# Fewer sums on TensorE, two scratch tiles for the dots and a shorter one-hot in a sparse graph attention layer

## The chip, the cores and the metric

The kernel runs on one core of a Trainium2 chip. The metric is the device time of one execution in microseconds (us). Several executions were timed, and one more was recorded by the hardware profiler; all times inside an execution come from that record and count from its first instruction.

## The reference

Input `x` has 3327 rows of 1024 fp32 values, `adj` is a 3327 x 3327 matrix of 0 and 1 (int32) with ones on its diagonal and few ones elsewhere (the chance of an edge is 0.0024 in each direction). The three weights are 1024 x 1024.

```python
h = jnp.maximum(_layernorm(x, axis=-1), 0.0)
f = h @ Wf + bf
g = h @ Wg + bg
e = relu(f @ g.T)
scores = jnp.where(adj > 0, e, NEG)
attention = softmax(scores, axis=1)
out = x + attention @ (h @ W + bW)
```

## The kernel before

Only the neighbours of a row count, since all other scores are NEG. The kernel uses two identities: `f @ g.T` equals `(h A + v) . h` for a product `A = Wf Wg^T` made once (with the biases in `v` and in one more column), and `attention @ (h W)` equals `(attention @ h) W`. So each row needs a query `q = h A + v` (TensorE), a dot product of `q` with the row `h` of each neighbour (VectorE), a softmax over these few scores, the weighted sum `y` of the same neighbour rows, and `y W`.

**First part (to about 237 us).** `adj` and `x` are streamed tile by tile (128 rows). ScalarE counts degrees, GpSimd multiplies `adj` by column numbers, VectorE extracts the neighbour lists with its max-of-8 operation, ScalarE normalizes `x` to `h`, and SP stores `h` (`hd`), the lists (`pd`) and the candidates (`cd`) to DRAM. TensorE computes `A` meanwhile. Rows are then sorted by degree: a one-hot of the rank's low seven bits (`ohp`, L1064 to L1073) is multiplied on TensorE with the high bits and gives the permutation `perm`, so that a tile holds rows of like degree. The one-hot is built in three pieces on VectorE, with the int32 `lo` and the fp32 `iotap` as operands, and the 26 matmuls follow piece by piece. After the second piece the last two tiles of `h` are scaled and stored, and the load of the last two of eight 512 KB pieces of `W_sb` is queued on SP. Then two gathers on GpSimd fetch the `h` rows of the first two tiles (`hps`, L1092), and the queries of these tiles are made (L1108 to L1122): three `bank` matmuls, transposes, and `third`, which makes 342 columns of `q` in 16 passes. After that come the last lists and stores.

**Second part.** The 26 tiles run in the order `ORDER`; tile t has `CAPS[ORDER[t]]` neighbour slots (37 down to 11, in all 468). The slots of a tile come in one or two chunks (`split`). The steps of a tile, with the functions that issue them (L1200 to L1344):

- `L`, `G`, `H`: GpSimd gathers the list, one 512 KB block of neighbour rows per slot k into one of 26 buffers `G`, and the tile's own rows. `H` is transposed (`turned`, `hc`) and multiplied with `A` (`third`, then `qc` copies to `q`, and `fq` refills the PSUM bank).
- `d` (L1247): one VectorE operation multiplies a neighbour block by `q` and accumulates the score of slot k. It also has to write the 128 x 1024 products somewhere: the tile `junk`, one for all dots. The operation is two instructions, the product and a read of the accumulator.
- `S`, `A`, `E`, `Y`, `T`: maximum, exponentials and sum of a chunk; `Y` scales slot 0, which becomes the running sum `y`.
- The weighted sum of the other slots goes two ways. On VectorE, `s` (L1299) does `y = G_k * w_k + y`. On TensorE, `w` (ScalarE) scales the block in place, and `p` (L1295) adds its transpose into PSUM by eight 128 x 128 transposes. `SHARE[t]` says how many slots of tile t go to TensorE (`on_tensor`), in all 185. At the end `yt` adds the transpose of `y` to the same PSUM banks, column half by column half, and `yc` copies to `yT`.
- `fo`, `W`, `rc`, `X`, `O`: bias, the projection on TensorE (32 passes), scaling, the added `x` and the scatter to the output.

The order on each engine in this part is written out by a planner in Python (`steps_of`, `forward`, `backward`, `planned`). `steps_of` lists every step with its engine, the time it takes and lasts, and what it depends on; `forward` plays the list with priorities, each engine taking the step of best rank (VectorE with a penalty `TURNS` for a second step of the same kind), and `backward` makes new ranks from the latest times. Of 30 passes with random jitter `WIDE` the best is kept, and the kernel issues the steps in the order of their planned start times. The semaphores between the engines come from the tiles that are read and written, not from the plan.

Of the kernel before, what the change touches and what calls it, by code (L numbers as in the profile page):

```python
# [10 lines left out]
FP = mybir.dt.float32  # L11
# [20 lines left out]
ORDER = [24, 15, *range(15), *range(16, 24), 25]  # L32
SHARE = [10, 12, 18, 13, 11, 10, 11, 9, 8, 8, 9, 9, 6, 9, 5, 4, 5, 4, 3, 3, 3, 2, 3, 0, 6, 4]
ONE_CHUNK = 18
# [7 lines left out]
SEED = 1  # L42
WIDE = 0.6
LAG = 2
# [284 lines left out]
def steps_of():  # L329
# [9 lines left out]
    for t, s in enumerate(ORDER):  # L339
# [3 lines left out]
        if t > 1:  # L343
            add("POOL", 1.31, 1.31, ("H", t), row=True)
            add("DMA", 1.33, 3.2, ("Hd", t), ("H", t))
            for g in range(2):
                add("PE", 0.44, 0.66, ("hT", t, g), ("Hd", t), ("hc", t - 1, g), ("hT", t, g - 1), frees=[("H", t)] * g)
            for g in range(2):
                add("ACT", 0.49, 0.6, ("hc", t, g), ("hT", t, g), *(("q", t - 1, i, j) for i in range(3) for j in range(QS)))
            for i in range(3):  # L350
                for j in range(QS):
                    add(
                        "PE", 4.66 / QS, 4.66 / QS + 0.2, ("q", t, i, j), ("hc", t, 0), ("hc", t, 1), ("fq", 3 * t + i),
                        ("q", t, i, j - 1),
                    )
                add(
                    "ACT", 0.4, 0.52, ("qc", t, i), ("q", t, i, QS - 1),
                    *(("d", t - 2, k) for k in range(CAPS[ORDER[t - 2]])),
                )
                if 3 * t + i + 2 < 3 * n:  # L360
                    add("ACT", 0.38, 0.48, ("fq", 3 * t + i + 2), ("qc", t, i))
# [6 lines left out]
        if t == n - 1:  # L368
            add("POOL", 1.31, 1.31, ("x", t), row=True)
            add("DMA", 1.33, 3.2, ("xd", t), ("x", t))  # L370
        summed = []
        for c, (k0, k1) in enumerate(ends):
            last = c == len(ends) - 1
            for k in range(k0, k1):
                late = [("F", t)] if k >= KL else [("hc", 2, 1) if k < 6 else ("qc", 2, 1)] if t == 1 else []
                add("POOL", 1.31, 1.31, ("G", t, k), ("Ld", t), *late, row=True)
                add("DMA", 1.33, 3.2, ("Gd", t, k), ("G", t, k))
                add(
                    "DVE", 1.2, 1.38, ("d", t, k), ("Gd", t, k), *(("qc", t, i) for i in range(3)),
                    ("M", t), at=(256.0, 266.0)[t] if t < 2 else 0.0,  # L380
                )
# [9 lines left out]
            for k in range(max(k0, 1), k1):  # L391
                if k in on_tensor(t):
                    add("ACT", 1.05, 1.15, ("w", t, k), ("E", t, c))
                    add("PE", 0.873, 1.07, ("p", t, k), ("w", t, k), ("yc", t - 1, 0), ("yc", t - 1, 1), frees=[("G", t, k)])
                    summed.append(("p", t, k))
                else:
                    add("DVE", 1.2, 1.28, ("s", t, k), ("E", t, c), ("Y", t, c), frees=[("G", t, k)])
                    summed.append(("s", t, k))
        for o in range(2):
            add("ACT", 0.62, 0.72, ("fo", t, o), ("rc", t - 1, o), ("T", t, len(ends) - 1))  # L400
        for g in range(2):
            add(
                "PE", 0.44, 0.66, ("yt", t, g), *summed, ("Y", t, len(ends) - 1), ("yc", t - 1, 0), ("yc", t - 1, 1),
                ("yt", t, g - 1),
                frees=[("G", t, 0)] * g,
            )
        for g in range(2):
            add("ACT", 0.49, 0.6, ("yc", t, g), ("yt", t, g), *(("W", t - 1, o, j) for o in range(2) for j in range(WS)))
        for o in range(2):
            for j in range(WS):  # L410
                add(
                    "PE", 7.0 / WS, 7.0 / WS + 0.2, ("W", t, o, j), ("yc", t, 0), ("yc", t, 1), ("fo", t, o),
                    ("W", t, o, j - 1),
                )
# [16 lines left out]
def forward(steps, rows, noise=None, fixed=None):  # L431
# [19 lines left out]
    while events:  # L451
# [7 lines left out]
        for e in FREE_AT:  # L459
# [24 lines left out]
            if e == "PE" and now < 480:  # L484
                takes, lasts = takes * 1.12, lasts * 1.12
            if e == "DVE":
                if k.name[0] in "ds" and k.name[0] == done:
                    takes, lasts = takes + 0.12, lasts + 0.12
                done = k.name[0]
# [86 lines left out]
def edge_path(ctx: ExitStack, tc: tile.TileContext, x, adj, Wf, bf, Wg, bg, W, bW, out, flag):  # L576
# [67 lines left out]
    with ExitStack() as part1:  # L644
# [212 lines left out]
        with tc.manual_schedule(engines={  # L857
# [59 lines left out]
            for i in range(NT - 3):  # L917
                degrees(i + 2)
                keys(i + 2, nc.gpsimd)
                if i == NT - 4:  # L920
                    degrees(NT - 1)
                    keys(NT - 1, nc.gpsimd)
                if i < 3:
                    for c in (2 * i + 2, 2 * i + 3):
                        transposed(WgT[:, :, c * P : (c + 1) * P], A_sb[:, c, :D])
                        empty()
# [91 lines left out]
            slots = slots.rearrange("p (t s) -> p t s", s=NT)  # L1018
            ohp = kpool.tile([P, N], FP, name="r").bitcast(BF)[:, : NT * P].rearrange("p (t d) -> p t d", d=P)

# [18 lines left out]
            lo = c1.tile([P, NT], I32, name="lo")  # L1039
            nc.vector.tensor_scalar(lo, ranki, P - 1, None, op0=ALU.bitwise_and)  # L1040
            measured(22, False)
            rooted(22)
# [20 lines left out]
            ps = p_mm.tile([P, CB], FP, name="ps_A")  # L1063
            for t0, t1 in ((0, 10), (10, 20), (20, NT)):  # L1064
                nc.vector.tensor_tensor(
                    ohp[:, t0:t1, :], lo[:, t0:t1, None].to_broadcast([P, t1 - t0, P]),
                    iotap[:, None, :].to_broadcast([P, t1 - t0, P]), op=ALU.is_equal,
                )
                for t in range(t0, t1):
                    nc.tensor.matmul(  # L1070
                        ps[:, : 2 * NT], ohp[:, t, :], place[:, t, :, :].rearrange("p a s -> p (a s)"),
                        start=(t == 0), stop=(t == NT - 1),
                    )  # L1073
                if t1 == 20:
                    inverted(late)
                    scaled(late)
                    store_h(late)
                    inverted(last)
                    scaled(last)
                    store_h(last)  # L1080
                    for k in range(6, KD):
                        load_W(k)
            listed(NT - 3)
# [25 lines left out]
            hTs = [wT.tile([P, KD, P], FP, name="WfT") for s in ORDER[:2]]  # L1109
            pq = [bank(i, True) for i in range(3)]  # L1110
            transposed(hTs[0], hps[0])
            empty()
# [19 lines left out]
            store_lists(last, NT)  # L1132
            store_left(last)

            over = c1.tile([P, 1], FP, name="over")
# [21 lines left out]
    with tc.manual_schedule(engines={  # L1157
# [9 lines left out]
        res = tiles("xp", 2, [P, O])  # L1167
        junk = tiles("junk", 1, [P, D], BF)[0]
        scs = tiles("sc", 3, [P, KM])
# [77 lines left out]
        def dot(t, k):  # L1247
            q = qs[t % 2]
            nc.vector.tensor_tensor_reduce(  # L1249
                junk, row(t, k), q[:, :D], 1.0, 0.0, op0=ALU.mult, op1=ALU.add,  # L1250
                accum_out=scs[t % 3][:, k : k + 1],
# [46 lines left out]

        def s(t, k):  # L1299
            y = row(t, 0)  # L1300
            nc.vector.scalar_tensor_tensor(y, row(t, k), scs[t % 3][:, k : k + 1], y, op0=ALU.mult, op1=ALU.add)  # L1301

# [98 lines left out]
```

## Time and profile before

| | |
|---|---|
| median of 3 executions (lowest, highest) | 1243.65 us (1237.1, 1246.98) |
| the profiled execution: its time, its span | 1243.08 us, 1241.3 us |
| TensorE busy, share of the span | 1117.1 us, 90% |
| VectorE (DVE) busy | 1108.0 us, 89% |
| GpSimd (POOL) busy | 895.3 us, 72% |
| ScalarE (ACT) busy | 618.3 us, 50% |
| read from HBM, over the span | 344.11 MB, 301 GB/s |
| mean granted TensorE clock | 0.953 |

The profile has several views. The slices cut the span into 40 parts of 31 us and give each engine's busy share in tenths; PEclk is the clock granted to TensorE in tenths of full speed. A line of the groups gives a source line, engine and operation, the tiles as out<-in, shapes, the count, busy time and mean ns of one, and then the idle time of the engine just before these instructions with what ended it. A line of the timeline gives start, duration, engine, source line, operation, tiles and, in brackets, the idle time before it and its releaser. PE is TensorE's matmuls, PEld its weight loads. The ends of matmuls are modelled, so that a busy TensorE isn't TensorE at its peak.

### The profile page before, as it was taken

The page shows a single profiled execution, that of the slowest core. Times are in us where ns is not written, and L with a number is a line of the kernel's source. Part 1 is how long each engine was busy: PE and PEld are TensorE (multiplying, and loading weights), DVE is VectorE, ACT ScalarE, POOL GpSimd, SP SyncE. Part 2 cuts the span into 40 slices and gives each one's busy share as a digit, 9 for nine tenths or more (in the row PEclk, how much of TensorE's full clock was granted, in tenths as well). Part 3 has the DMA queues.
Part 4 walks back from the last instruction along what each step waited for, and adds up shares of the span by engine and source line. Part 5 has one row for each costly group of instructions (what it writes and reads, how often), then busy time and mean ns, then how long its engine had stood idle before and what let it go on. Part 6 is the DMA issues. An engine that isn't in the chain of part 4 may idle for free. (4 is left out here: it accounts for less than half of the span.)

```text
span 1241.3 us, 14490 instructions
## 1 busy us (share of the span) xinstructions
PE 1117.1 (90%) x4632; PEld 712.1 (57%) x4632; DVE 1108.0 (89%) x2169; ACT 618.3 (50%) x941; POOL 895.3 (72%) x676
## 2 busy tenths in 40 slices
PE   2799980779998899999999999999999999999995
PEld 1566650447647466566666676665666565655553
DVE  5999997638898989988999999998999999999991
ACT  6899988216526275346543565453323433333250
POOL 8999994355676777776777777657777887777721
PEclk8799995789998899999999999999999999999998
DMA  9999999677868999998999989779988999899842
GB/s 368 419 396 397 403 344 354 199 297 265 293 222 271 312 338 303 316 324 294 303 337 332 310 292 330 274 248 317 319 289 274 317 305 319 267 313 314 301 137 53
DMA packets 101916, 374.46 MB, mean 302 GB/s; under 512 B 14859, under 2 KB 18602, under 8 KB 98631
## 3 DMA queue, kind: packets, MB, share of 16 engines
q0 software_dynamic: 79584, 286.77, 68.8%
q1 hardware_dynamic: 22246, 86.68, 18.5%
q8 instruction: 38, 0.62, 0.2%
q14 instruction: 48, 0.39, 0.1%
HBM read 344.11 MB, written 29.30 MB: 301 GB/s over the span
## 5 line engine op out<-in xcount | busy, mean ns | idle before, releaser
L635 POOL DMA_INDIRECT G<-hd,ps x454 | 535.8, 1180 | 207.1 <-issue 99.3
L1249 DVE CUSTOM_DVE_ANT_0 junk<-G,q 128x1024 bf16<-128x1024 f32 x468 | 573.4, 1225 | 58.1 <-ACT q L1120 26.8
L1316 PE MATMUL p_o<-W_sb,yT 128*128 128x512 f32 x832 | 365.4, 594 | 1.1 <-ACT yT L1312 0.9
L1236 PE MATMUL p_q<-A_sb,hT 128*128 128x342 f32 x1152 | 356.5, 459 | 6.6 <-ACT hT L1232 2.9
L1301 DVE SCALAR_TENSOR_TENSOR G<-G,sc 128x1024 f32<-128x1024 f32 x257 | 330.8, 1287 | 9.2 <-ACT G L1274 4.1
L1236 PEld LDWEIGHTS p_q<-A_sb,hT 128*128 128x128 f32 x1152 | 215.8, 193 | 113.3 <-issue 15.1
L1316 PEld LDWEIGHTS p_o<-W_sb,yT 128*128 128x128 f32 x832 | 156.6, 190 | 190.1 <-issue 183.7
L1289 PE MATMUL p_y<-ident,G 128*128 128x128 f32 x1688 | 207.2, 274 | 15.8 <-issue 10.9
L1289 PEld LDWEIGHTS p_y<-ident,G 128*128 128x128 f32 x1688 | 190.0, 141 | 47.1 <-issue 25.4
L1285 ACT ACTIVATE G<-G,sc 128x1024 f32<-128x1024 f32 x185 | 197.2, 1138 | 0.1
L700 POOL TENSOR_TENSOR r<-r,iotaj 128x1664 f32<-128x1664 f32 (+3 forms) x50 | 183.7, 3729 | 3.9 <-ACT r L693 3.9
L1327 ACT ACTIVATE xp<-p_o,rs 128x512 f32<-128x512 f32 x50 | 33.0, 682 | 201.6 <-DMA out_dram<-xp,perm 97.9
L833 PE MATMUL ps_A<-WgT,WfT 128*128 128x342 f32 x432 | 129.3, 458 | 2.4 <-ACT WfT L828 2.4
L763 DVE MAX8 cand<-r 128x8 f32<-128x208 f32 (+2 forms) x416 | 118.9, 360 | 3.8 <-POOL r L700 3.5
L833 PEld LDWEIGHTS ps_A<-WgT,WfT 128*128 128x128 f32 x432 | 81.1, 191 | 42.3 <-ACT WfT L828 2.6
L1242 ACT COPY q<-p_q 128x342 f32<-128x342 f32 x72 | 31.7, 445 | 105.5 <-DVE sc L1249 46.8
L693 ACT ACTIVATE r<-r 128x3327 f32<-128x3327 int32 (+3 forms) x27 | 77.3, 2864 | 11.6 <-DMA r<-in_adj_dram 11.6
L1312 ACT COPY yT<-p_y 128x512 f32<-128x512 f32 x52 | 30.1, 584 | 68.9 <-PE p_y L1289 58.2
L635 POOL DMA_INDIRECT xp<-in_x_dram,perm x25 | 44.0, 1760 | 17.9 <-ACT xp L1327 11.2
L1334 POOL DMA_INDIRECT out_dram<-xp,perm x25 | 32.2, 1286 | 31.3 <-DMA xp<-in_x_dram,perm 20.7
L1232 ACT COPY hT<-p_t 128x512 f32<-128x512 f32 x48 | 27.3, 586 | 54.1 <-PE p_q L1236 23.6
L1270 ACT ACTIVATE sc<-sc,nm 128x10 f32<-128x10 f32 (+10 forms) x36 | 11.0, 305 | 81.2 <-DVE nm L1260 39.7
(144 smaller groups left out, 715.1 us busy)
## 6 DMA issues: line engine op xcount, KB each, us to landing
r<-in_adj_dram SPq DMA_DIRECT2D x24, 1663.5 KB, 12.2
xt<-in_x_dram SPq DMA_DIRECT2D x22, 512.0 KB, 13.3
hd<-xt SPq DMA_DIRECT2D x22, 512.0 KB, 10.5
G<-hd,ps POOLq DMA_INDIRECT x454
A_sb<-in_L_gnn_Wg_dram SPq DMA_DIRECT2D x8, 512.0 KB, 17.1
A_sb<-in_L_gnn_Wf_dram SPq DMA_DIRECT2D x8, 512.0 KB, 11.9
W_sb<-in_L_gnn_W_dram SPq DMA_DIRECT2D x8, 512.0 KB, 7.8
cd<-cand SPq DMA_DIRECT2D x25, 64.0 KB, 12.7
```

Of the source, the lines that this page charges most:

```text
L635: return nc.gpsimd.indirect_dma_start(out=to, out_offset=None, in_=table, in_offset=bass.IndirectOffsetOnAxis(ap=idx, axis=0), **kw,)
L693: nc.scalar.activation(r[:n, b:e], a[:n, b:e], AF.Sign, accum_out=to)
L700: eng.tensor_mul(r[:n, b:e], r[:n, b:e], iotaj[:n, b:e])
L763: nc.vector.max(cands[t][:n, s * 8 : s * 8 + 8], r[:n, s * SW : min(N, (s + 1) * SW)])
L833: nc.tensor.matmul(ps[:, :QB], WfTs[c][:, k, :], WgT[:, k, o : o + QB], start=(k == 0), stop=(k == KD - 1))
L1236: nc.tensor.matmul(ps_q[(3 * t + i) % 2][:, :QB], hT[:, k, :], A_sb[:, k, i * QB : (i + 1) * QB], start=False, stop=(k == KD - 1), skip_gr ...
L1249: nc.vector.tensor_tensor_reduce(junk, row(t, k), q[:, :D], 1.0, 0.0, op0=ALU.mult, op1=ALU.add, accum_out=scs[t % 3][:, k : k + 1],)
L1285: nc.scalar.activation(g, g, AF.Copy, scale=scs[t % 3][:, k : k + 1])
L1289: nc.tensor.matmul(ps_y[g][:, c, :], of[:, (4 * g + c) * P : (4 * g + c + 1) * P], ident, is_transpose=True, start=((t, g) not in begun an ...
L1301: nc.vector.scalar_tensor_tensor(y, row(t, k), scs[t % 3][:, k : k + 1], y, op0=ALU.mult, op1=ALU.add)
L1316: nc.tensor.matmul(ps_o[o], yT[:, k, :], W_sb[:, k, o * CB : (o + 1) * CB], start=False, stop=(k == KD - 1), skip_group_check=True,)
L1327: nc.scalar.activation(to, ps_o[o], AF.Copy, scale=rss[t % 3])
```

## The change

- `SHARE` moves slots from TensorE (`w` and `p`) to VectorE (`s`): the list's sum falls from 185 to 168, one slot each in 17 tiles.
- `junk` becomes `junks`, two tiles; dot k writes tile k % 2.
- In the last tile `s` works on one column half at a time, so that the transposes of the first half depend on the sums of the first half alone.
- The planner's table follows: a dot takes 1.148 in place of 1.2, the surcharge of 0.12 for two operations of a kind in a row remains for sums alone, TensorE is no longer taken as 12% slower before 480 us, `WIDE` is 0.3, and `qc` and `W` get the dependencies that the diff shows. So the order of the second part is computed anew.
- The one-hot is one operation with bf16 operands: `lob` (a bf16 copy of `lo`) against `iotaq`, a constant that GpSimd writes in the first part. Its layout has the tile index innermost, and the 26 matmuls read their weights with that stride.
- The loads of the last two pieces of `W_sb` move behind the last lists and stores.
- Six matmuls of 512 columns whose result is not used (`warm`) stand between the three `bank` matmuls and the first transposes.

```diff
-SHARE = [10, 12, 18, 13, 11, 10, 11, 9, 8, 8, 9, 9, 6, 9, 5, 4, 5, 4, 3, 3, 3, 2, 3, 0, 6, 4]
+SHARE = [9, 11, 18, 12, 10, 9, 10, 8, 7, 7, 8, 8, 5, 8, 4, 4, 4, 4, 3, 3, 3, 2, 3, 0, 5, 3]
-WIDE = 0.6
+WIDE = 0.3
...
-                    *(("d", t - 2, k) for k in range(CAPS[ORDER[t - 2]])),
+                    *(("d", t - 2, k) for k in range(CAPS[ORDER[t - 2]])), *(("S", t - 2, c) for c in range(2) if i == 2),
...
-                    "DVE", 1.2, 1.38, ("d", t, k), ("Gd", t, k), *(("qc", t, i) for i in range(3)),
+                    "DVE", 1.148, 1.32, ("d", t, k), ("Gd", t, k), *(("qc", t, i) for i in range(3)),
...
+                elif t < n - 1:
+                    add("DVE", 1.205, 1.29, ("s", t, k), ("E", t, c), ("Y", t, c), frees=[("G", t, k)])
+                    summed.append(("s", t, k))
                 else:
-                    add("DVE", 1.2, 1.28, ("s", t, k), ("E", t, c), ("Y", t, c), frees=[("G", t, k)])
-                    summed.append(("s", t, k))
+                    for g in range(2):
+                        add("DVE", 0.66, 0.74, ("s", t, k, g), ("E", t, c), ("Y", t, c), ("s", t, k, g - 1), frees=[("G", t, k)] * g)
+                        halves[g].append(("s", t, k, g))
...
-                    "PE", 7.0 / WS, 7.0 / WS + 0.2, ("W", t, o, j), ("yc", t, 0), ("yc", t, 1), ("fo", t, o),
-                    ("W", t, o, j - 1),
+                    "PE", 7.0 / WS, 7.0 / WS + 0.2, ("W", t, o, j), *(("yc", t, g) for g in range(2 * (j + 1) // WS)),
+                    ("fo", t, o), ("W", t, o, j - 1),
...
-                takes, lasts = takes * 1.12, lasts * 1.12
+                takes, lasts = takes * 1.0, lasts * 1.0
             if e == "DVE":
-                if k.name[0] in "ds" and k.name[0] == done:
+                if k.name[0] == "s" == done:
...
+                    iotaq = c1.tile([P, P, NT], BF, name="iotaq")
+                    nc.gpsimd.iota(
+                        iotaq, pattern=[[1, P], [0, NT]], base=0, channel_multiplier=0,
+                        allow_small_or_imprecise_dtypes=True,
+                    )
...
+            lob = c1.tile([P, NT], BF, name="lob")
+            nc.vector.tensor_copy(lob, lo)
...
-            for t0, t1 in ((0, 10), (10, 20), (20, NT)):
-                nc.vector.tensor_tensor(
-                    ohp[:, t0:t1, :], lo[:, t0:t1, None].to_broadcast([P, t1 - t0, P]),
-                    iotap[:, None, :].to_broadcast([P, t1 - t0, P]), op=ALU.is_equal,
+            nc.vector.tensor_tensor(
+                ohp, lob[:, None, :].to_broadcast([P, P, NT]), iotaq, op=ALU.is_equal
+            )
+            for t in range(NT):
+                nc.tensor.matmul(
+                    ps[:, : 2 * NT], ohp[:, :, t], place[:, t, :, :].rearrange("p a s -> p (a s)"),
+                    start=(t == 0), stop=(t == NT - 1),
                 )
...
-                    for k in range(6, KD):
-                        load_W(k)
...
+            warm = p_tr.tile([P, 4, P], FP, name="ps_tr").rearrange("p a b -> p (a b)")
+            for i in range(6):
+                nc.tensor.matmul(warm, ident, A_sb[:, i, :CB], start=True, stop=True)
             transposed(hTs[0], hps[0])
...
+            for k in range(6, KD):
+                load_W(k)
...
-        junk = tiles("junk", 1, [P, D], BF)[0]
+        junks = tiles("junk", 2, [P, D], BF)
...
-                junk, row(t, k), q[:, :D], 1.0, 0.0, op0=ALU.mult, op1=ALU.add,
+                junks[k % 2], row(t, k), q[:, :D], 1.0, 0.0, op0=ALU.mult, op1=ALU.add,
...
-        def s(t, k):
-            y = row(t, 0)
-            nc.vector.scalar_tensor_tensor(y, row(t, k), scs[t % 3][:, k : k + 1], y, op0=ALU.mult, op1=ALU.add)
+        def s(t, k, g=None):
+            part = slice(0, D) if g is None else slice(g * CB, (g + 1) * CB)
+            y, row_k = row(t, 0)[:, part], row(t, k)[:, part]
+            nc.vector.scalar_tensor_tensor(y, row_k, scs[t % 3][:, k : k + 1], y, op0=ALU.mult, op1=ALU.add)
```

More of the change, by code (lines that the diff above doesn't have):

```diff
@@ L370, in steps_of @@
             add("DMA", 1.33, 3.2, ("xd", t), ("x", t))
-        summed = []
+        summed, halves = [], ([], [])
         for c, (k0, k1) in enumerate(ends):
@@ L402, in steps_of @@
             add(
-                "PE", 0.44, 0.66, ("yt", t, g), *summed, ("Y", t, len(ends) - 1), ("yc", t - 1, 0), ("yc", t - 1, 1),
+                "PE", 0.44, 0.66, ("yt", t, g), *summed, *halves[g], ("Y", t, len(ends) - 1), ("yc", t - 1, 0), ("yc", t - 1, 1),
                 ("yt", t, g - 1),
@@ L1018, in edge_path @@
             slots = slots.rearrange("p (t s) -> p t s", s=NT)
-            ohp = kpool.tile([P, N], FP, name="r").bitcast(BF)[:, : NT * P].rearrange("p (t d) -> p t d", d=P)
+            ohp = kpool.tile([P, N], FP, name="r").bitcast(BF)[:, : NT * P].rearrange("p (d t) -> p d t", t=NT)
             incl = c1.tile([P, NBIN], FP, name="incl")
@@ L1063, in edge_path @@
             ps = p_mm.tile([P, CB], FP, name="ps_A")
-            for t0, t1 in ((0, 10), (10, 20), (20, NT)):
-                nc.vector.tensor_tensor(
-                    ohp[:, t0:t1, :], lo[:, t0:t1, None].to_broadcast([P, t1 - t0, P]),
-                    iotap[:, None, :].to_broadcast([P, t1 - t0, P]), op=ALU.is_equal,
-                )
[L1069 to L1080, printed above, removed]
-                    for k in range(6, KD):
-                        load_W(k)
+            nc.vector.tensor_tensor(
[5 more added lines that the diff above has]
+                    start=(t == 0), stop=(t == NT - 1),
+                )
+            inverted(late)
+            scaled(late)
+            store_h(late)
+            inverted(last)
+            scaled(last)
+            store_h(last)
             listed(NT - 3)
```

## The prediction

> **What bounds the kernel now.** I read the page's slices first, then the costliest groups, then the timeline of VectorE, of the start and of the end. The slices show no single bound:
>
> ```profile
> PE   2799980779998899999999999999999999999995
> DVE  5999997638898989988999999998999999999991
> ...
> PEclk8799995789998899999999999999999999999998
> DMA  9999999677868999998999989779988999899842
> ```
>
> TensorE and VectorE are both over 90% busy from slice 19 (570 us) to the tail, and DMA is near 90%. As PE's ends are modelled, I price its work by start distances instead: 32 projection matmuls stand between 1196.06 and 1209.90, so 0.4325 each; 48 transposes take 5.40 us with 0.27 for the last, so 0.109 each; the 342-column matmuls 0.2875. Counted in the timeline, the stretch from 570 to 1210 holds 832 matmuls of `p_q`, 614 of `p_o` and 1145 transposes: 239.2+265.6+124.8 = 629.6 us of PE in 640. VectorE, by the distances shown below, needs 310 dots x1.148 + 193 sums x1.197 + 16.2 of small operations + 121 pairs of dots x0.119 + 27 pairs of sums x0.124 = 620.9. In the same way the 290 us from 280 on hold 248 of PE and 266 of VectorE: there both wait in turn. So **PE bounds the late stage with VectorE 9 us behind it**. The groups that the change touches:
>
> ```profile
> L1249 DVE CUSTOM_DVE_ANT_0 junk<-G,q 128x1024 bf16<-128x1024 f32 x468 | 573.4, 1225 | 58.1 <-ACT q L1120 26.8
> ...
> L1301 DVE SCALAR_TENSOR_TENSOR G<-G,sc 128x1024 f32<-128x1024 f32 x257 | 330.8, 1287 | 9.2 <-ACT G L1274 4.1
> ...
> L1289 PE MATMUL p_y<-ident,G 128*128 128x128 f32 x1688 | 207.2, 274 | 15.8 <-issue 10.9
> ...
> L1285 ACT ACTIVATE G<-G,sc 128x1024 f32<-128x1024 f32 x185 | 197.2, 1138 | 0.1
> ```
>
> VectorE's timeline shows what its 98% consists of:
>
> ```profile
> 707.81 1.22 DVE L1249 CUSTOM_DVE_ANT_0 junk<-G,q 128x1024 bf16<-128x1024 f32 x1
> 708.95 0.08 DVE L1249 DVE_READ_ACCUMULATOR2_ANT sc<- 128x1 f32 x1
> 709.07 1.22 DVE L1249 CUSTOM_DVE_ANT_0 junk<-G,q 128x1024 bf16<-128x1024 f32 x1
> 710.22 0.08 DVE L1249 DVE_READ_ACCUMULATOR2_ANT sc<- 128x1 f32 x1
> 710.22 1.28 DVE L1301 SCALAR_TENSOR_TENSOR G<-G,sc 128x1024 f32<-128x1024 f32 x1
> 711.41 1.22 DVE L1249 CUSTOM_DVE_ANT_0 junk<-G,q 128x1024 bf16<-128x1024 f32 x1
> ```
>
> A dot followed by a dot takes 1.26 us from start to start (median 1.267), one followed by a sum 1.15 (median 1.144), a sum followed by a dot 1.197, by a sum 1.321. The later dot starts after the accumulator read has ended, and every dot writes the one tile `junk`. Of 468 dots 204 are followed by another.
>
> In the start, VectorE stands still for want of the first queries:
>
> ```profile
> 224.97 1.09 POOL L635 DMA_INDIRECT xt<-hd,perm  x1 [24.05 <-DMA W_sb<-in_L_gnn_W_dram]
> ...
> 231.74 1.94 PE L817 MATMUL ps_tr<-ident,xt 128*128 128x128 f32 x8 [8.42 <-DMA xt<-hd,perm]
> ...
> 269.13 0.79 ACT L1120 COPY q<-ps_A 128x342 f32<-128x342 f32 x2 [15.90 <-remote]
> 269.61 1.23 DVE L1249 CUSTOM_DVE_ANT_0 junk<-G,q 128x1024 bf16<-128x1024 f32 x1 [26.77 <-ACT q L1120]
> ```
>
> The gather of the first rows needs 6.7 us to land while W_sb pieces 6 and 7 load (issued 220.44 and 221.44); the transposes behind it run at half clock (8 in 1.94 us; 1.03 for the next 8 at 240.81). From 255.8 to 268.4 PE starts only nine matmuls, at multiples of 0.7 us, for no reason that the trace names; the gathers run back to back then, at some 410 GB/s.
>
> [...]
>
> **The change part by part**, against the profiled execution (span 1241.3, 1.8 around it, 1243.1; the median of the three runs, 1243.65, is 0.6 above).
>
> *Slots.* The new list sums to 168, not the 167 of the words; I take the list. PE loses 17x8 transposes = 17x0.87 = 14.8 us, ACT 17x1.138 = 19 us (it is half idle, so nothing), VectorE gains 17 sums = 17x1.197 = 20.3.
>
> *Two scratch tiles.* If the wait on `junk` is the whole gap, 204x(1.267-1.148) = 24.3 us leave VectorE; 1.148 is what a dot takes before any other operation. Bounds: 0, if the accumulator read itself holds the next dot, to 24.3. I take 24.3, since small operations that start straight after the read do so without delay (24 such at 1.151). Net on VectorE: -4.
>
> *By stage.* Tiles 6 on finish after 570 us and lose 12 of the 17 slots. Late stage: PE 629.6-12x0.87 = 619; VectorE 620.9-121x0.119+12x1.197 = 620.9. The larger load falls from 629.6 to 620.9, so 8.7 is the most to gain, and what now stands between PE's need and the stage (10.4) must grow some with no slack left on either. I take -6 (-1 to -9). Early stage: PE -5x0.87 = -4.4, VectorE 5x1.197-75x0.119 = -2.9. I take -2 (0 to -4).
>
> *Last tile by halves.* Seven sums become 14. A half, from the 0.75 us row of 128x512 (`xp`), is 0.74 long and some 0.66 from start to start: 14x0.66 = 9.2, against 7x1.321 = 9.2 in a chain. The first half's transposes may start one half (0.7) earlier, but in before four slots of PE end at 1213.4 after the sums (1212.15), so PE hid it; with three slots the two meet. Zero (-0.7 to +1).
>
> *The planner's numbers* (dot 1.148, no surcharge for dot after dot, PE not 1.12 times slower before 480, a narrower jitter, two true dependencies): they only choose an order, which I can't see. The added edges are in the program already: W starts at 1196.06 while the second `yT` copy runs to 1196.49. Zero, +-4.
>
> *One-hot.* Three operations of 1.42, 1.42 and 0.94 us become one of 128x3328[...], from 212.2 to at most 215.9. VectorE waited until 216.23 for ACT's rstd anyway, so both cost the same, and what is saved is the third operation that stood behind that wait: -0.9, plus `lob` (0.1, in the wait of 0.94 at 210.09). The 26 matmuls follow in one go, 1.6 us before[...]. `iotaq` costs POOL about 3.0 us (iotaj's row), between 200.9 and 223.8, where it is idle. Stores of `hd` keep their time.
>
> *W_sb 6 and 7* move behind eight small SP stores. Those lists leave 1.4 us sooner, the gather of 225.0 gets the bandwidth (-2), and the 1 MB falls beside the row gathers from 236 on: 3 us at 336 GB/s, on a queue that VectorE isn't yet waiting for. W is first read at 308; `bWb`, behind them, at about 285, is landed by then.
>
> *Six warm matmuls.* Twelve passes of 0.43 us (0.86 at half clock), from 223.3 to 228.5 (233.6), inside the idle 8.4 us; queued behind are the transposes, which ACT's WfT copies and the thirds wait for. At full clock they pay back 0.9 (transposes), 1.0 (bank) and about 3 in the first thirds. If the clock isn't granted they cost 2.
>
> *Start in sum*: gather 2, clock 4-5, VectorE 0.9, or some 8 us, if the stretch of nine matmuls is no worse than before. Bounds: +2 (warm at half clock) to -16 (all 48 matmuls of the first query are over before the gathers crowd: VectorE starts at about 253, as rows land). I take -8; all that follows moves with it, since PE goes straight from the thirds into tile 2.
>
> Sum: 1243.1 - 8 - 2 - 6 = **1227**.
>
> **The rivals.** *(a) The start hardly moves*: the stall ends with the last gathers at 268-269 whatever came before. For it: it ends as DMA drains. Start -2: 1233. *(b) The balance gives it back*: PE and VectorE both at 620, a new order that starves one in turn, as in the early stage; only the start's -3 stays: 1240. For it: the early stage loses 8% with both under 92%. *(c) Slower*: the gap between dots is not `junk`'s. Then VectorE carries 897+20.3 = 917 us of work between 270 and 1210 (897 from 467 dots, 256 sums and 203 pairs, priced as above), where 43 us are lost to waits already; with those kept it ends 20 later: 1243+20-3 = 1260. It decides from where two tiles save under 20.3/204 = 0.10 us a pair. Against it: operations of one input start right after the read. *(d) The stall vanishes*: start -16: 1219.
>
> **How the numbers follow.** Forecast 1227: 0.46; (a) 0.2; (b) 0.14; (c) 0.1; (d) 0.1. Eight in ten: from 1212 (part of (d) lies below) to 1244, leaving (c) out. A measurement of this kernel tells about 1% from no change, 12.4 us: faster means under 1231.2. The forecast, (d) and a quarter of (a) give 0.46+0.1+0.05 = 0.61; the rest of (a) and (b) 0.15+0.14 = 0.29; slower is (c), 0.10.
>
> **What would show it.** Dot to dot at 1.15 instead of 1.267; `p_y` matmuls at 1552; VectorE's first dot near 260; transposes at full speed near 229; PE at 0.98 of its need from 570 on. Wrong if dots keep 1.26, if the wait for `q` stays above 20 us, or if VectorE's idle time grows late.

## The result and the profile after

| | before | after |
|---|---|---|
| median of 20 executions (lowest, highest) | 1245.03 us (1237.1, 1260.24) | 1235.75 us (1231.33, 1246.55) |
| ratio after to before, 95% interval | | 0.9927 (0.9905 to 0.9949) |
| profiled execution: its time, its span | 1243.08, 1241.3 | 1233.38, 1231.6 |
| TensorE, VectorE, GpSimd busy | 1117.1, 1108.0, 895.3 | 1099.2, 1120.3, 936.7 |
| first half of `yT` copied for the first, the seventh, the last tile in the order, at | 308, 588, 1214 | 297, 570, 1204 |
| second half, at | 309.3, 590.3, 1214.5 | 297.6, 584.2, 1204.5 |

The change gains 0.7%: less than the forecast (1227), inside its range (1212 to 1244). The gain is small: on one chip, below, the kernel before differed from itself by 0.6%. All ratios here leave disturbed executions out, and so need not equal the quotient of two medians. The slices of the kernel after, in tenths of 31 us each:

```profile
PE   2799990799939899999999999999899999999995
...
DVE  5999998758898999998999999999999999999991
...
PEclk9899995799979999999999999999999999999998
DMA  9999999589788999989899899888998999998942
```

TensorE now has a slice of 3 (339 to 370 us) where it had 9; both engines are over 90% busy in most slices after 600 us, as before. The groups of the kernel after (busy and mean ns, then idle time before them):

```profile
L639 POOL DMA_INDIRECT G<-hd,ps x454 | 567.4, 1250 | 159.2 <-issue 107.0
L1260 DVE CUSTOM_DVE_ANT_0 junk<-G,q 128x1024 bf16<-128x1024 f32 x468 | 563.9, 1224 | 34.0 <-DMA G<-hd,ps 19.2
...
L1313 DVE SCALAR_TENSOR_TENSOR G<-G,sc 128x1024 f32<-128x1024 f32 (+1 forms) x281 | 354.5, 1262 | 6.8 <-ACT G L1285 3.7
...
L1300 PE MATMUL p_y<-ident,G 128*128 128x128 f32 x1552 | 190.1, 275 | 12.7 <-DVE G L1313 6.8
```

The slots moved as planned: 1552 transposes, 281 sum operations (274 sums, seven of them in halves). New in this list is GpSimd's row gather, 1250 ns on average where it took 1180. The timeline of the kernel after shows a slow one under a dot (255.82), and what the start became (start, duration, engine, line, operation, and the idle time before it):

```profile
200.95 5.30 POOL L928 IOTA iotaq<- 128x3328 bf16 x1
...
201.74 4.56 DVE L1032 TENSOR_SCALAR incl<-incl 128x48 f32<-128x48 f32 x1
...
215.92 1.84 DVE L1075 TENSOR_TENSOR r<-lob,iotaq 128x3328 bf16<-128x3328 bf16 x1
...
233.91 1.94 PE L821 MATMUL ps_tr<-ident,xt 128*128 128x128 f32 x8 [5.24 <-DMA xt<-hd,perm]
...
243.60 23.17 PE L1109 MATMUL ps_A<-A_sb,WfT 128*128 128x342 f32 x80
...
255.78 1.22 DVE L1260 CUSTOM_DVE_ANT_0 junk<-G,q 128x1024 bf16<-128x1024 f32 x1
255.82 1.99 POOL L639 DMA_INDIRECT G<-hd,ps  x1 [0.30 <-issue]
256.92 0.08 DVE L1260 DVE_READ_ACCUMULATOR2_ANT sc<- 128x1 f32 x1
256.92 1.22 DVE L1260 CUSTOM_DVE_ANT_0 junk<-G,q 128x1024 bf16<-128x1024 f32 x1
258.07 0.08 DVE L1260 DVE_READ_ACCUMULATOR2_ANT sc<- 128x1 f32 x1
258.07 1.22 DVE L1260 CUSTOM_DVE_ANT_0 junk<-G,q 128x1024 bf16<-128x1024 f32 x1
```

- A dot now follows a dot after 1.15 us, before the read of the accumulator has ended: the wait was `junk`'s. The trace holds the opposite case too. The tile goes by the slot number (`k % 2`), but the plan doesn't issue the slots in the order of k, so 33 of the 179 dots that follow a dot write the same tile as the dot before (by the order that the kernel's planner gives). These start at least 1.255 us after it (median 1.264); of the other 146 the median is 1.146.
- In return a gather issued under such dots can take 1.99 instead of 0.94 us; 102 of 492 take 1.9 or more, before 49.
- VectorE's small `incl` operation takes 4.56 instead of 0.19 us, as long as GpSimd's iota runs. It stands on the way to `perm`, which comes at 223.1 in place of 220.2, the first gather at 229.0 in place of 225.0.
- The stretch of nine matmuls at multiples of 0.7 us is gone: 80 matmuls run in one piece, the first dot starts at 253.5 (before 269.6), the transposes of the third tile at 270.4 (before 280.1).

Where did the time come from? The kernel after is 10 us ahead when the third tile starts (270.4 against 280.1) and 10 us ahead at the last `yT`. In between no tile is a clean mark, since the two orders differ: at the seventh tile the lead is 18 us by the first half of `yT` and 6 by the second, at the tenth it is 2. What is sure is the whole: from the third tile's transposes to the last `yT` both kernels take 934 us (933.9 and 933.7), although TensorE needs 14.8 us less in the kernel after. So the start gives the 10, and what the second part saved was given back. My first reading was that the start's stretch of slow issue was avoided by the new start, and that the slower gathers ate the gain of the second part. Both had to be tried.

### The profile page after: what moved, and what is told of

Same layout as the page of the kernel before. It is cut to its first block, busy times and chain, and to the rows that moved or that the text cites. A ratio compares the mean times of both kernels' runs of the same rounds, so it can differ in the third digit from the quotient of the medians.

```text
span 1231.6 us, 14006 instructions
## 1 busy us (share of the span) xinstructions
PE 1099.2 (89%) x4508; PEld 697.5 (57%) x4508; DVE 1120.3 (91%) x2192; ACT 602.7 (49%) x924; POOL 936.7 (76%) x677
## 5 line engine op out<-in xcount | busy, mean ns | idle before, releaser
L639 POOL DMA_INDIRECT G<-hd,ps x454 | 567.4, 1250 | 159.2 <-issue 107.0
L1260 DVE CUSTOM_DVE_ANT_0 junk<-G,q 128x1024 bf16<-128x1024 f32 x468 | 563.9, 1224 | 34.0 <-DMA G<-hd,ps 19.2
L1313 DVE SCALAR_TENSOR_TENSOR G<-G,sc 128x1024 f32<-128x1024 f32 (+1 forms) x281 | 354.5, 1262 | 6.8 <-ACT G L1285 3.7
L1247 PE MATMUL p_q<-A_sb,hT 128*128 128x342 f32 x1152 | 350.5, 455 | 7.8 <-ACT p_q L1256 5.7
L1300 PE MATMUL p_y<-ident,G 128*128 128x128 f32 x1552 | 190.1, 275 | 12.7 <-DVE G L1313 6.8
L1300 PEld LDWEIGHTS p_y<-ident,G 128*128 128x128 f32 x1552 | 175.0, 142 | 40.8 <-issue 15.3
L1296 ACT ACTIVATE G<-G,sc 128x1024 f32<-128x1024 f32 x168 | 179.2, 1138 | 0.1
L697 ACT ACTIVATE r<-r 128x3327 f32<-128x3327 int32 (+3 forms) x27 | 77.3, 2865 | 10.2 <-DMA r<-in_adj_dram 10.2
```

The lines of the kernel that those rows point to most:

```text
L639: return nc.gpsimd.indirect_dma_start(out=to, out_offset=None, in_=table, in_offset=bass.IndirectOffsetOnAxis(ap=idx, axis=0), **kw,)
L697: nc.scalar.activation(r[:n, b:e], a[:n, b:e], AF.Sign, accum_out=to)
L1247: nc.tensor.matmul(ps_q[(3 * t + i) % 2][:, :QB], hT[:, k, :], A_sb[:, k, i * QB : (i + 1) * QB], start=False, stop=(k == KD - 1), skip_gr ...
L1260: nc.vector.tensor_tensor_reduce(junks[k % 2], row(t, k), q[:, :D], 1.0, 0.0, op0=ALU.mult, op1=ALU.add, accum_out=scs[t % 3][:, k : k + 1],)
L1296: nc.scalar.activation(g, g, AF.Copy, scale=scs[t % 3][:, k : k + 1])
L1300: nc.tensor.matmul(ps_y[g][:, c, :], of[:, (4 * g + c) * P : (4 * g + c + 1) * P], ident, is_transpose=True, start=((t, g) not in begun an ...
```

## The experiments

Ratios are to the kernel before, timed alongside on the same chip. The three groups ran on three chips, called 11, 4 and 13 here.

### The parts, on chip 11 (the kernel before: 1250.82 us)

**The first part alone**: the kernel before with the new one-hot, `iotaq`, the later loads of `W_sb` and the warm matmuls.

> The kernel before with the edits of the first part alone (one-hot with iotaq and lob, W_sb 6 and 7 late, six warm matmuls); slots, scratch tile and order of the second part as before. Theory A, all of the 9 us comes from the start, where TensorE reaches tile 2 at 270.4 in place of 280.1, and the second part keeps its length: 9 to 10 us below before. Rival B, the second part is held by other things and takes an earlier start back, and the gain is that of the slots: 0 to 4 us below before.

**The second part alone**: the changed kernel with the first part of before.

> The changed kernel with the first part as before: fewer slots on TensorE, two scratch tiles, halves and the new plan alone. Theory A: within 3 us of before, since VectorE's load is the same as before (24.3 us of gaps out, 20.3 us of sums in). Rival B: 6 to 9 us below before.

**One scratch tile**, all else changed:

```diff
-        junks = tiles("junk", 2, [P, D], BF)
+        junks = tiles("junk", 1, [P, D], BF)
...
-                junks[k % 2], row(t, k), q[:, :D], 1.0, 0.0, op0=ALU.mult, op1=ALU.add,
+                junks[0], row(t, k), q[:, :D], 1.0, 0.0, op0=ALU.mult, op1=ALU.add,
```

> The changed kernel with one scratch tile in place of two, order unchanged. 179 dots follow a dot in the changed kernel; with one tile each starts 0.117 us later, 21 us in all. Theory A, VectorE sets the length of the second part: 15 to 21 us above the changed kernel, slower than before. Rival, TensorE sets it and VectorE has slack: 0 to 6 us above.

**`iotaq` early**: the iota of L928 moved ahead of GpSimd's scaling of `bgT`, at some 10 us.

```diff
+            iotaq = c1.tile([P, P, NT], BF, name="iotaq")
+            nc.gpsimd.iota(
+                iotaq, pattern=[[1, P], [0, NT]], base=0, channel_multiplier=0,
+                allow_small_or_imprecise_dtypes=True,
+            )
             nc.gpsimd.tensor_scalar(WgT[:, :, D], bgT, -1.0, None, op0=ALU.mult)
...
-                    iotaq = c1.tile([P, P, NT], BF, name="iotaq")
-                    nc.gpsimd.iota(
-                        iotaq, pattern=[[1, P], [0, NT]], base=0, channel_multiplier=0,
-                        allow_small_or_imprecise_dtypes=True,
-                    )
```

> The changed kernel with iotaq written at about 10.5 us, where GpSimd waits for bgT and then for ScalarE, in place of 201. Theory: in the changed kernel the write of 5.30 us holds VectorE's scalar operation at 201.74 for 4.4 us, and all that follows starts 4 us later; 3 to 4 us below the changed kernel, and that operation takes 0.2 us. Rival: the delay is swallowed by waits that follow: within 1 us of the changed kernel.

| chip 11 | median (executions) | ratio (interval) | first dot | third tile's transposes | dot to dot | gather |
|---|---|---|---|---|---|---|
| first part alone | 1251.44 (22) | 0.9971 (0.9941, 1.0001) | 253.6 | 278.0 | 1.267 | 1.200 |
| second part alone | 1237.48 (9) | 0.9915 (0.9878, 0.9953) | 265.3 | 280.3 | 1.147 | 1.258 |
| changed, one scratch tile | 1278.54 (6) | 1.0134 (1.0059, 1.0209) | 251.2 | 267.2 | 1.267 | 1.210 |
| changed, `iotaq` early | 1232.65 (6) | 0.9882 (0.9829, 0.9935) | 250.3 | 267.2 | 1.150 | 1.265 |

The gap between dots and the gathers' length follow the number of scratch tiles in every row: this is settled. Without the second tile the ratio is 1.0134, against 0.9927 for the change in the record: some 26 us (the intervals leave 14 to 38), more than the 21 us of the gaps. I put the rest to the plan, which was made for dots of 1.148 and gives VectorE 17 more sums; this wasn't taken apart and isn't shown. The iota's hold is settled too: moved away, `incl` takes 0.19 us. What it costs is not: the third tile's transposes start 3.2 us sooner than in the record, but as soon in the row above, where the iota stands late and `incl` takes 3.61 us; the total moves by less than the intervals tell.

The second part alone keeps the whole gain (0.9915), where I had expected to be within 3 us of before.

The first part alone didn't do what I had read into it: 0.3% instead of 9 to 10 us. Its first dot comes 16 us sooner than in the profile shown with the prediction (the kernel before was not traced on chip 11), yet the third tile's transposes gain 2: the slow issue stands a little later in the program. The timeline of this kernel:

```profile
269.21 0.59 PE L1191 MATMUL p_q<-A_sb,ident 128*128 128x512 f32 x1 [0.83 <-issue]
270.61 0.59 PE L1193 MATMUL p_o<-A_sb,ident 128*128 128x512 f32 x1 [0.81 <-issue]
272.71 0.71 PE L1193 MATMUL p_o<-A_sb,ident 128*128 128x512 f32 x1 [1.51 <-issue]
274.11 1.01 PE L1191 MATMUL p_q<-A_sb,ident 128*128 128x512 f32 x1 [0.69 <-issue]
```

Again the starts are multiples of 0.7 us apart, and the profile shows nothing late that these matmuls need: the idle time is put to "issue". So the new start doesn't avoid this stretch. I had a second guess, that it comes from gathers issued back to back, which the second scratch tile slows.

### What avoids the slow issue, on chip 4 (the kernel before: 1218.52 us)

**The changed kernel again.**

> The changed kernel itself once more, as the mark for the others on this chip: 0.9927 times before, 8 to 10 us below it. If the stretch in which TensorE issues one instruction in 0.70 us is left out by what the change does and not by chance, it is absent from this profile too.

**The kernel before with two scratch tiles** and nothing else of the change.

> The kernel before with two scratch tiles alone, slots and order as before. Dots that follow dots start after 1.15 in place of 1.267 (204 of them, 24 us of VectorE's load). TensorE sets the second part: 0 to 5 us below before, since its load stays. VectorE sets it: 10 to 20 us below. The stretch of slow issue on TensorE near 256 to 268 stays, as VectorE has no work there.

**The changed kernel with the old slots**: `SHARE` of before (185), planned anew with the new numbers.

> The changed kernel with the old list of 185 slots on TensorE, order planned for it. TensorE carries 14.8 us more, VectorE 20.3 less. If TensorE would then set the late stage, as I held for before: 5 to 10 us above the changed kernel. If VectorE or something else sets it: 0 to 10 us below.

**The kernel before with paced gathers**: one scratch tile, and GpSimd kept busy with a 128x512 memset after each gather of the first two tiles.

```diff
             gather(row(t, k), hd[:, :], entry(t, k))
+            if t < 2:
+                nc.gpsimd.memset(pace, 0.0)
```

> The kernel before with a small GpSimd operation (512 fp32 zeros to a tile that nothing reads) behind each gather of the first two tiles, so that these gathers are issued at some 1.9 us in place of 1.24. Theory S, the slow issue on TensorE comes of gathers back to back that fill the DMA queues: the stretch from 255.8 to 268.4 is gone, VectorE's first dot comes at 252 to 258 in place of 269.6, and the time is 3 to 10 us below before. Rival, it is tied to the place in the program or to the clock: the stretch stays, and the time is 0 to 5 us above before.

| chip 4 | median (executions) | ratio (interval) | third tile's transposes | seventh `yT` | last `yT` | gather |
|---|---|---|---|---|---|---|
| changed | 1233.81 (6) | 1.0125 (1.0101, 1.0149) | 269.6 | 573 | 1209 | 1.278 |
| before, two scratch tiles | 1222.67 (22) | 1.0033 (1.0018, 1.0048) | 265.7 | 566 | 1198 | 1.240 |
| changed, old slots | 1249.11 (5) | 1.0257 (1.0235, 1.0278) | 269.3 | 575 | 1218 | 1.267 |
| before, paced gathers | 1231.77 (5) | 1.0110 (1.0089, 1.0131) | 266.7 | 577 | 1203 | 1.209 |

This group turned the result round. On this chip the kernel before takes 1218.5 us, 2.6% less than on chip 11, and **the change makes it slower by 1.25%**. None of the four traces has the slow stretch, the one with quick gathers as little as the others, so the pacing test tells nothing of its cause; the pacing itself costs 13 us. Two readings follow. Two scratch tiles alone don't pay under the old order (+0.3%, where I had expected 0 to 5 us less). In that order 83 of the 204 dots that follow a dot write the same tile as the dot before and stay at 1.267, so 14 of the 24 us of gaps could go. These seem to have gone into waits, TensorE bounding that order: dots wait 22.8 us for gathers, and VectorE ends early and waits 15.4 us for the last projection. The changed kernel with fewer slots is 15.3 us under the one with the old list; each has an order of its own, so this isn't the slots' price alone.

### The chip or the order, on chip 13 (the kernel before: 1249.19 us)

**The kernel before again**, for its trace; it was not traced on chip 4.

> The kernel before once more, for a second trace of it on another chip. Theory L (the level of the kernel before differs by chip because the stretch of slow issue at multiples of 0.70 us in its start is there on some chips and not on others): if its runs here lie near 1218 us, the trace shows no such stretch, the first dot near 250 and the transposes of the third tile near 266; if they lie near 1245 to 1250, the stretch is there again and these are at 265 to 270 and 280. Rival (the level differs throughout): the start is the same in both, and every tile of the second part takes some 2% less or more.

**The changed kernel with the planner's old numbers:**

```diff
-WIDE = 0.3
+WIDE = 0.6
...
-                    "DVE", 1.148, 1.32, ("d", t, k), ("Gd", t, k), *(("qc", t, i) for i in range(3)),
+                    "DVE", 1.2, 1.38, ("d", t, k), ("Gd", t, k), *(("qc", t, i) for i in range(3)),
...
-                    add("DVE", 1.205, 1.29, ("s", t, k), ("E", t, c), ("Y", t, c), frees=[("G", t, k)])
+                    add("DVE", 1.2, 1.28, ("s", t, k), ("E", t, c), ("Y", t, c), frees=[("G", t, k)])
...
-                takes, lasts = takes * 1.0, lasts * 1.0
+                takes, lasts = takes * 1.12, lasts * 1.12
...
-                if k.name[0] == "s" == done:
+                if k.name[0] in "ds" and k.name[0] == done:
```

> The changed kernel with the planner's numbers of before (a dot 1.2, a surcharge for dots too, TensorE 12% slower before 480 us, the wider jitter), all else kept: slots, two scratch tiles, halves, start. Theory P (the new numbers order the second part worse, and this ate what the slots and the scratch tiles gave): 10 us or more under the changed kernel in the same call, 1215 to 1224. Rival Q (the order is worth nothing; the late stage is held by GpSimd's slower gathers and by both engines at their need): within 4 us of the changed kernel.

**The same with `iotaq` early.**

> The last one, and iotaq written at 10 us, where it holds nothing, in place of 201 us. With theory P 2 to 4 us under the run with the old numbers alone, and the fastest of all, near 1215; with Q within 2 us of it, since a start that is 3 us earlier was lost by the third tile when the iota alone was moved.

**The changed kernel a third time.**

> The changed kernel on this chip, for comparison. By theory L its own time is 1232 to 1238 on every chip, and only the kernel before moves: a ratio of 0.99 where the kernel before has the slow stretch, 1.012 where it has not. Rival: the changed kernel moves along with the kernel before, and the ratio stays near 0.993.

| chip 13 | median (executions) | ratio (interval) | third tile's transposes | seventh `yT` | last `yT` |
|---|---|---|---|---|---|
| before | 1253.02 (12) | 1.0061 (1.0025, 1.0097) | 279.6 | 588 | 1223 |
| changed, old numbers | 1259.78 (6) | 1.0108 (1.0057, 1.0159) | 275.4 | 602 | 1232 |
| the same, `iotaq` early | 1255.13 (8) | 1.0110 (1.0070, 1.0150) | 261.6 | 590 | 1223 |
| changed | 1241.92 (22) | 0.9965 (0.9936, 0.9995) | 266.8 | 581 | 1219 |

The first row compares the kernel before with itself: 0.6% with an interval that excludes 1. Its trace has the slow stretch in the start again, as I had expected at this level (first dot at 268.3). So gaps of this size are not to be read on this chip, and the last row's 0.35% with them.

**The level goes with slow issue.** I summed TensorE's idle time that the profile puts to "issue" in each profiled execution. For the kernel before again, TensorE's waits (total, times, longest) of this kind are

```profile
PE p_y L1289 <- issue: 9.8, 15, 1.2
PE ps_A L1103 <- issue: 8.3, 7, 2.1
...
PE p_t L1229 <- issue: 5.4, 2, 5.1
...
PE p_q L1236 <- issue: 2.9, 7, 0.7
```

or 26.4 us, and 22.4 in the profile shown with the prediction (spans 1250.6 and 1241.3). For the others: first part alone 23.8, second part alone 13.2, one scratch tile 17.0, `iotaq` early 3.6; the changed kernel 8.0 in the record and 24.6 on chip 13; with old numbers 6.4 and 16.7. **In all four traces of chip 4 it is 0.0.** So on chips 11 and 13, and on the record's, TensorE is now and then held without a cause that the trace shows, in different amounts from one execution to the next, and on chip 4 it isn't. This goes together over three chips; no run changed it alone. The kernel before, less its 22.4 or 26.4, comes to 1219 and 1224, near its 1218.5 on chip 4. The subtraction doesn't hold in general: 1231.6 less 8.0 is 1224 for the changed kernel, which takes 1233.8 with none.

How much is held isn't measured by this sum. "Issue" means that no release was recorded, and the traces differ in that. The pages of the kernel before and of the changed kernel on chip 4 have these lines for the gathers:

```profile
G<-hd,ps POOLq DMA_INDIRECT x454
...
G<-hd,ps POOLq DMA_INDIRECT x454, 6.1
```

The second gives the time to landing, the first can't: of the 11504 records of a DMA's progress that a full trace has, the four of chip 4 have all, and the ten others lack 1883 to 3016. Nor is TensorE alone in it. ScalarE's idle time without a known releaser ("issue" or "remote") is 58 to 137 us in the ten, and 7.9, 0, 0 and 0 on chip 4. What stands without this label are the starts at multiples of 0.7 us, since the matmuls are all recorded.

In its third run the changed kernel isn't spared; it meets the slow issue after the start. Its timeline on chip 13:

```profile
293.63 0.38 PE L1300 MATMUL p_y<-ident,G 128*128 128x128 f32 x2 [1.00 <-issue]
...
294.37 0.27 PE L1240 MATMUL p_t<-ident,G 128*128 128x128 f32 x1 [0.25 <-issue]
295.09 0.42 PE L1240 MATMUL p_t<-ident,G 128*128 128x128 f32 x2 [0.45 <-issue]
295.81 0.94 PE L1300 MATMUL p_y<-ident,G 128*128 128x128 f32 x4 [0.30 <-issue]
...
303.81 0.59 ACT L1243 COPY hT<-p_t 128x512 f32<-128x512 f32 x1 [15.80 <-remote]
...
304.55 0.59 ACT L1324 COPY yT<-p_y 128x512 f32<-128x512 f32 x1 [0.15 <-remote]
...
305.19 5.07 PE L1328 MATMUL p_o<-W_sb,yT 128*128 128x512 f32 x6 [8.44 <-issue]
```

On chip 4 these projections start at 294.59 with no wait. The 8.44 us are not TensorE's own: they end with ScalarE's copy of `yT`, and ScalarE had stood until 303.81 for a signal of unknown source, though the transposes that it then copied start at 291.73. In this trace 17.2 of the 24.6 us end just as an operation of ScalarE or VectorE ends whose result the matmul uses. The first tile's `yT` comes at 305, against 294 on chip 4: 11 us of the start's lead are lost. So my expectation of 1232 to 1238 on every chip was wrong too.

**The order is not free.** With the same slots and tiles, the planner's old numbers give 1259.8 where the new give 1241.9, 18 us apart (1.4% by the ratios). I had guessed the opposite sign: the new numbers would be what ate the gain. With `iotaq` early as well the ratio stays (1.0110). In the old numbers' order 68 of 172 dots after a dot share its tile, in the new one 33 of 179; at 0.12 us each that is 4 us of VectorE. The old numbers' order also leaves a hole, which its timeline shows:

```profile
385.09 1.97 PE L1240 MATMUL p_t<-ident,G 128*128 128x128 f32 x8 [28.41 <-DMA G<-hd,perm]
```

TensorE stands 28.4 us for the gather of a tile's own rows (`H`), which GpSimd issues at 379.76, behind the gathers that the plan put first. The order of the changed kernel has a smaller one, in the slice marked 3 above:

```profile
361.81 1.68 POOL L639 DMA_INDIRECT G<-hd,perm  x1 [0.67 <-DVE G L1313]
...
368.04 1.97 PE L1240 MATMUL p_t<-ident,G 128*128 128x128 f32 x8 [18.75 <-DMA G<-hd,perm]
```

Of the six gathers that GpSimd issues from 350.01 on, three wait for a buffer that a sum on VectorE frees, and five take 1.4 to 1.7 us; `H` stands in the queue behind them. The 8 transposes then run at half clock (granted 0.50; 1.97 us, in before 1.04). It is there in the changed kernel on chips 4 and 13 as well (16.9 and 10.2 us), so it belongs to the order. In the profile of before, `H` costs TensorE 6.4 us in all, in this one 23.6. What an order without this hole would take was not tried. No run beat both kernels clearly: `iotaq` early has the lowest ratio on its chip (0.9882), but the record's interval for the change overlaps its own.

## Why the prediction was right, and where not

**Dots and slots: right.** Dot to dot 1.150 (forecast 1.15), 1552 transposes, and rival (c), a gap that isn't `junk`'s, is out. The 24.3 us took every pair of dots for two different tiles; 33 pairs share one, so some 20 us go ((204 - 33) x 0.119). That the same edit slows gathers was missing in the sum: the mean of 492 row gathers goes from 1.196 to 1.256 us, 29 us of GpSimd. In the profile of after, the 30 gathers that start while VectorE runs neither a dot nor a sum all take about 0.94 us; of the 341 that start under a dot 99 take 1.9 or more, of the 121 under a sum 3. Why a gather under a dot can take so long isn't shown. The share of the slower gathers in the total is not isolated; two scratch tiles under the old order cost 4 us net on chip 4, less than the 0.6% by which the kernel before differed from itself on chip 13.

**Start, -8: the size is right and the reasons are wrong.** The third tile's transposes came 9.7 sooner. But

- "gather 2": the first rows land sooner after their gather, as forecast (the transposes follow it by 4.9 us, before by 6.8), but the gather came 4.0 later. The failing step is "`iotaq` costs POOL about 3.0 us where it is idle": it takes 5.3 and holds VectorE 4.4; by what means isn't shown. With the iota early the gather comes at 225.8.
- "clock 4-5": none of it before the first thirds. The warm matmuls end at 228.7, the rows land 5.24 us later, and the transposes run at half clock as before (8 in 1.94 us, granted clock 0.50). Where the wait is 2.49 (old numbers, `iotaq` early), 8 transposes take 1.06 us, and the thirds start at 229.4 instead of 237.3. So it can go either way in one kernel: in the changed kernel's run on chip 13 the wait is 3.02 and the transposes take 1.07. The longer waits are followed by the slow transposes: 5.24 us in the record, 5.27 with the first part alone and 6.54 with `iotaq` early, each time with 8 transposes in 1.94 us.
- "VectorE 0.9": the one-hot is one operation of 1.84 us, where the three of before took 3.78, but it starts at 215.92, pushed by the iota; `perm` is 2.9 later.
- What gave the gain is the stretch of slow issue, absent in this execution. On chip 4, where no trace has it, the third tile of the changed kernel comes 3 to 4 us later than in the two kernels with the old start. I had this as rival (d) at 0.10, as an effect of timing. The first part alone kept the stretch, and the changed kernel had as much slow issue on chip 13 as the kernel before. So the record's gain rests in part on how much of it an execution meets.

**Early and late stage, -2 and -6: together 0.** From the third tile's transposes to the last `yT`, TensorE's need, priced as in the prediction, fell from 881.9 to 867.1 us, and the rest of the time, unfilled, rose from 52.0 to 66.6. Up to 570 us that is 41.6 and 42.7, in spite of the `H` hole, since before has slow issue there (at 403 to 413, 460 and 501 to 504). From 570 to 1210 the need fell from 629.6 to 616.1 and VectorE's busy time from 617.3 to 614.0, but "PE at 0.98 of its need from 570 on" became 0.963: 23.9 us unfilled in place of 10.4. The failing step is "**PE bounds the late stage with VectorE 9 us behind it**", taken as if both kept their fill. The waits of TensorE in this stretch of the kernel after:

```profile
PE p_y L1300 <- DVE G L1313: 6.8, 3, 5.3
PE p_y L1300 <- ACT G L1296: 2.7, 2, 2.5
```

It now waits 6.8 us for sums on VectorE (before 2.2) and 2.7 for scaled blocks, and VectorE 9.0 us for gathers in place of 4.6. This is rival (b), balance given back, and it happened together with the start's gain. Whether the order or the slower gathers did it isn't separated.

**The planner's numbers, "zero, +-4": wrong in size.** Old against new numbers: 18 us. On chip 4, the step from two scratch tiles alone to the whole change less its slots is 26 us worse. That step also holds the first part, which sets the third tile 3.6 later; the rest is the order and the halves. By these two steps the term for a new order should have been some +-20 (an estimate), more than the 14.8 us that the slots take from TensorE.

**Halves of the last tile, zero: right.** 14 halves take 10.61 us (0.76 each, forecast 0.66); TensorE's transposes still end 1.6 us after the last sum, in before 2.3.

**The sum**: -8, -2, -6 forecast; -10 and, for the two stages together, 0 found. The total was near by luck: the start's gain came of a stretch that some executions meet and some don't. By chip, the change is worth -0.7% in the record, nothing that can be told on chip 13, where both kernels meet slow issue alike (24.6 and 26.4 us), and +1.25% on chip 4, where there is none.

## What to carry to other kernels

When an order is written by a planner, price "planned anew" from runs of several orders, and look first for a long wait of one engine on a single gather. A wait on a scratch tile between two operations can be removed by a second tile (here from 1.267 to 1.150 us from dot to dot), but let the tiles alternate in the order of issue and not by an index, and ask who else slows down with it: here GpSimd's gathers did (1.196 us on average before, 1.256 after). A big constant belongs where VectorE does nothing in a chain (here writing it held VectorE for 4.4 us), and a comparison of 1% that was made on one chip should be repeated on another before it is believed.

## What the runs showed that I had not expected

- The same kernel takes 1218.5 us on one chip and 1249 to 1251 on two others, each from 27 to 35 executions. TensorE's idle time by "issue" is 0.0 in the four traces of the first, and 3.6 to 26.4 in the eight of the others, which also lack records.
- The slow stretches recur at similar places of the program. In the two traces of the kernel before they begin after 727 and 731 matmuls, 1315 and 1299, 1552 and 1546. In two of the three traces of the changed kernel's orders on chip 13 they stand after 914 to 924 and 1043 to 1054 (with the old numbers alone in neither). No run changed what could lie behind them, and it isn't tested whether the recording itself plays a part. The cause stays open.
- A GpSimd iota of 128x3328 bf16 held a VectorE operation of 0.19 us for 4.4 us.
